# A spline layer on one Trainium2 core: two image tiles made one, and a masked sum moved from TensorE to GpSimd

## The chip, the cores and the metric

The kernel runs on one core of a Trainium2 chip. A core has four compute engines that work side by side and meet only through semaphores: PE (TensorE, matrix products into PSUM), DVE (VectorE), ACT (ScalarE) and POOL (GpSimd). SP (SyncE) starts DMAs. The metric is the device time of one whole execution in microseconds (us), smaller is better. Three runs of the kernel before took 19758.29, 19760.24 and 19772.59 us, a median of 19760.24 us.

## The reference, cut to what matters

The input `x` is (8, 64, 128, 128) in fp32. Four layers follow one another, each as `x = x + layer(group_norm(x))`. The first compares patches with weights by sums of absolute differences, the third is a wavelet convolution, the fourth replaces every pixel's 64 channels by the nearest of 512 vectors. The change is in the second, layer 1, a spline per channel:

```python
def _L1_conv_ref(x, coef, scale_base, scale_sp, bias):
    grid = _extended_grid(x.dtype)            # 12 knots, -2.2 to 2.2, 0.4 apart
    xcl = jnp.moveaxis(x, 1, -1)
    basis = _bspline_basis(xcl[..., None], grid)   # cubic, 8 functions
    spline = jnp.einsum('bhwck,ck->bhwc', basis, coef)
    out = scale_base * jax.nn.silu(xcl) + scale_sp * spline + bias
    return jnp.moveaxis(out, -1, 1)
...
x = x + _L1_conv_ref(_gn(x), L1_conv_coef, L1_conv_scale_base, L1_conv_scale_sp, L1_conv_bias)
```

## The kernel before, in words

Two images at a time make a pair: 128 partitions are 2 images of 64 channels. There are four pairs. Layer 0 of a pair is the bulk of the time; layers 2 and 3 of the pair before are threaded into layer 0 of the next one by a hand-written order. Layer 1 stands alone between two layer 0s (`run`, L1213), so it is a stage of its own, four times in the program. In the last pair, layers 2 and 3 follow it alone.

Inside layer 1 the order of instructions is not written out by hand. The framework orders them before the program runs, and each engine then works through its own queue in that fixed order. An instruction that waits holds back all that is behind it on its engine.

A stage handles 16 units (the loop at L719) of 8 rows, that is `N` = 1024 numbers per partition. For a unit:

- `xd` holds each image twice, on both halves of the partitions, as loaded by four DMAs from SP (L683). The lower half of the partitions serves three of six knots, the upper half the other three, so that one instruction makes two knots. For each of the two images ACT makes `z` = |2.5 (x - mean) / std| (L730), in a tile of 1024 columns.
- For each of three knot pairs `p` and each image `i`: `r` is the distance to the knot, cut at zero, made by ACT as a Relu (L739; `p` < 1 + `i`, which is three of the six) or by DVE as a min and a subtraction (L741; the other three, with the opposite sign). ACT squares it into `r3` (L742), and DVE multiplies `r3` by `r` (L743), which makes the cube.
- PE sums the cubes with the spline's coefficients into two PSUM tiles of 2 banks (L754): `pa` holds the part that counts everywhere, `pb` what is added where x is right of the mean. Each product has 64 output columns; the two images go to the two halves of the array and run side by side. A product in fp32 shows as two MATMUL instructions in the profile.
- ACT also makes `sl`, a Silu (L748), which PE adds to `pa` with the base scale (L756).

`end(n, pa, pb)` (L704) finishes a unit, called one unit late, at `p` = 1 of the next unit. DVE makes `u` = (x >= mean) * `pb` (L708). PE adds `u` to `pa` with two products by the identity, that is four instructions (L710). DVE then adds `pa`, the bias and `x` in place into `x` (L711). After every second unit DVE takes four `bn_stats` (L408) for the next group norm, and, but in the last pair, SP stores the chunk (L716).

PSUM has eight banks, all in use: `pa` and `pb` have two buffers of two banks. In SBUF, in buffers of 1024 columns: `z0` and `z1` two each, `r` three, `r3` five, `sl` two, `u` one.

Outside layer 1, POOL also copies borders between tiles in layer 2 of the last pair (L798, L799), while DVE does additions and subtractions there (L805 to L811).

Of the kernel before, what the change touches and what calls it, by code (L numbers as in the profile page):

```python
# [13 lines left out]
F32 = mybir.dt.float32  # L14
U32 = mybir.dt.uint32
AF = mybir.ActivationFunctionType
ALU = mybir.AluOpType
# [4 lines left out]
P = 128  # L22
# [8 lines left out]
NQ = 6  # L31
# [64 lines left out]
class Net:  # L96
# [568 lines left out]
    def layer1(self, mr, stats, store):  # L665
        nc, tc = self.nc, self.tc
        N = R * W // 2
        images = [slice(i * C, (i + 1) * C) for i in range(2)]
        with ExitStack() as ctx:
            sp = ctx.enter_context(tc.tile_pool(name="l1", bufs=2))  # L670
            xdp = ctx.enter_context(tc.tile_pool(name="l1_xd", bufs=3))
            cp = ctx.enter_context(tc.tile_pool(name="l1_c", bufs=1))
            pp = ctx.enter_context(tc.tile_pool(name="l1_ps", bufs=2, space=PSUM))

            def unit(n):
                return self.x[n // 2][:, n % 2 * R // 2 : (n % 2 + 1) * R // 2, :].rearrange("p r w -> p (r w)")

            def twice(n):

                xd = xdp.tile([P, 2, N], F32, name="xd")  # L680
                for i in range(2):
                    for h in range(2):
                        nc.sync.dma_start(out=xd[images[h], i, :], in_=self.x_of[0][images[i], n * N : (n + 1) * N])  # L683
                if n % 2 == 0:
                    self.x.append(self.load(n // 2))
                return xd

            l1w = cp.tile([P, L1W], F32, name="l1w")
            nc.sync.dma_start(out=l1w, in_=self.l1w_dram)
            dspl = l1w[:, 0 : 10 * C].rearrange("p (k n c) -> p k n c", k=2, n=5)  # L690
            dbase, of_image = l1w[:, 10 * C : 12 * C], l1w[:, 12 * C :].rearrange("p (i n) -> p i n", i=2)
            self.x = []
            xds = [twice(n) for n in range(3)]

            sb = cp.tile([P, 2], F32, name="sb")
            nc.vector.tensor_copy(sb[:, 0:1], mr[:, 1:2])
            nc.vector.tensor_scalar(sb[:, 1:2], mr[:, 0:1], mr[:, 1:2], -1.0, ALU.mult, ALU.mult)
            zb = cp.tile([P, 2, 2], F32, name="zb")
            for i in range(2):
                pm = pp.tile([P, 2, 512], F32, name="pm", tag="pa")  # L700
                nc.tensor.matmul(pm[:, 0, 0:2], of_image[:, i, :], sb, start=True, stop=True)
                nc.vector.tensor_scalar(zb[:, i, :], pm[:, 0, 0:2], 2.5, None, ALU.mult)

            def end(n, pa, pb):  # L704

                xv = unit(n)
                u = sp.tile([P, N], F32, name="u", bufs=1)
                nc.vector.scalar_tensor_tensor(u, xv, mr[:, 0:1], pb.rearrange("p q n -> p (q n)"), ALU.is_ge, ALU.mult)  # L708
                for q in range(2):
                    nc.tensor.matmul(pa[:, q, :], self.ident, u[:, q * 512 : (q + 1) * 512], start=False, stop=True)  # L710
                nc.vector.scalar_tensor_tensor(xv, pa.rearrange("p q n -> p (q n)"), self.bias1, xv, ALU.add, ALU.add)  # L711
                if n % 2 == 1:
                    j = n // 2
                    self.chunk_stats(stats, j)
                    if store:
                        nc.sync.dma_start(out=self.x_of[1][:, j * R * W : (j + 1) * R * W], in_=self.x[j].rearrange("p r w -> p (r w)"))  # L716

            late = None
            for n in range(2 * NCH):  # L719
                xv = unit(n)  # L720

                def work(name, bufs=2):
                    return sp.tile([P, N], F32, name=name, tag=name, bufs=bufs)

                pa = pp.tile([P, 2, 512], F32, name="pa")
                pb = pp.tile([P, 2, 512], F32, name="pb")
                zs = []
                for i in range(2):
                    z = work(f"z{i}")
                    nc.scalar.activation(z, xds[n][:, i, :], AF.Abs, bias=zb[:, i, 1:2], scale=zb[:, i, 0:1])  # L730
                    zs.append(z)
                for p in range(NQ // 2):
                    cubes, ws = [], []
                    for i in range(2):
                        r, r3 = work("r", 3), work("r3", 5)
                        kn = self.knots[:, p : p + 1]
                        on_act = p < 1 + i
                        if on_act:
                            nc.scalar.activation(r, zs[i], AF.Relu, bias=kn, scale=-1.0)  # L739
                        else:  # L740
                            nc.vector.tensor_scalar(r, zs[i], kn, kn, ALU.min, ALU.subtract)  # L741
                        nc.scalar.activation(r3, r, AF.Square)  # L742
                        nc.vector.tensor_tensor(r3, r3, r, ALU.mult)  # L743
                        cubes.append(r3)
                        ws.append(p + 3 if on_act else p)
                    if p == 0:
                        sl = work("sl")
                        nc.scalar.activation(sl, xv, AF.Silu, bias=sb[:, 1:2], scale=sb[:, 0:1])  # L748
                    for q in range(2):
                        cols = slice(q * 512, (q + 1) * 512)  # L750
                        for k, to in enumerate((pa, pb)):
                            for i in range(2):
                                stop = k == 1 and p == NQ // 2 - 1
                                nc.tensor.matmul(to[images[i], q, :], dspl[:, k, ws[i], :], cubes[i][:, cols], start=(p == 0), stop=stop)  # L754
                        if p == 1:
                            nc.tensor.matmul(pa[:, q, :], dbase, sl[:, cols], start=False, stop=False)  # L756
                    if p == 1 and late is not None:
                        end(*late)
                late = (n, pa, pb)
                if n + 3 < 2 * NCH:  # L760
                    xds.append(twice(n + 3))
                if n in range(4, 12, 2) and not store:
                    k = n // 2 - 2
                    nc.sync.dma_start(out=self.w2[:, k], in_=self.w2_dram[:, k])
            end(*late)

# [485 lines left out]
```

## Time and profile before

| what | us |
|---|---|
| median of three runs | 19760.24 |
| the profiled execution, its own time | 19757.03 |
| its span, first to last instruction | 19755.3 |
| PE busy in the span | 18769.1 |
| DVE busy | 18064.8 |
| ACT busy | 17182.7 |
| POOL busy | 2601.9 |
| layer 1, first to last product, pair 1 | 235.3 (3819.8 to 4055.1) |
| pair 2 | 238.8 (8699.2 to 8938.0) |
| pair 3 | 238.8 (13573.5 to 13812.3) |
| pair 4 | 236.1 (18435.9 to 18672.0) |

The four stages of layer 1 come to 949.0 us, 4.8% of the span; whatever the page says of busy shares over the span is mostly about layer 0, so layer 1 is read by windows of its own. A line of a group reads: line of the code, engine, operation, output <- inputs with their shapes, number, then busy time of the group in us and mean duration of one in ns, then how long the engine had been idle before and which instruction ended that. A line of the timeline reads: start in us, duration in us, engine, line, operation, and in brackets the idle time before it.

### The profile page before, as it was taken

How to read it: one execution, taken by the hardware profiler on the slowest of the kernel's cores; microseconds unless marked ns; L12 is line 12 of the kernel's file. 1: busy time of each engine (PE TensorE's matmuls, PEld its weight loads, DVE VectorE, ACT ScalarE, POOL GpSimd, SP SyncE). 2: the span in 40 equal slices, each digit the busy share in tenths (PEclk: the TensorE clock that was granted, in tenths of full speed). 3: DMA queues.
4: the chain of work that ended last, by engine and by line, in shares of the span. 5: the costliest groups of instructions: out<-in, count | busy, mean ns of one | idle time of the engine just before them, and what ended most of it. 6: DMA issues, size and time to landing. Idle time of an engine off the chain costs nothing. (4 is left out here: it accounts for less than half of the span.)

```text
span 19755.3 us, 326806 instructions
## 1 busy us (share of the span) xinstructions
PE 18769.1 (95%) x145178; PEld 5842.9 (30%) x145178; DVE 18064.8 (91%) x13865; ACT 17182.7 (87%) x6359; POOL 2601.9 (13%) x1726
## 2 busy tenths in 40 slices
PE   8999999999999999999999999999999999999898
PEld 2323323222222222222222222222222222222243
DVE  8999999989999899988999989998899999899837
ACT  7999999889899999988989999997999999999603
POOL 0000000000000333200000033310000003331004
PEclk9999999999999999999999999999999999999996
DMA  1000000211111000021111100002111110000101
GB/s 51 10 6 10 8 10 10 63 44 34 40 34 32 14 23 22 25 76 33 33 38 34 32 17 19 24 26 81 31 31 37 33 31 18 22 21 16 57 1 35
DMA packets 412631, 583.91 MB, mean 30 GB/s; under 512 B 64080, under 2 KB 309456, under 8 KB 385744
## 3 DMA queue, kind: packets, MB, share of 16 engines
q1 hardware_dynamic: 353872, 495.80, 8.4%
q0 software_dynamic: 57344, 67.21, 1.9%
q8 instruction: 1137, 18.63, 0.4%
q14 instruction: 278, 2.28, 0.0%
HBM read 439.55 MB, written 123.25 MB: 28 GB/s over the span
## 5 line engine op out<-in xcount | busy, mean ns | idle before, releaser
L589 ACT ACTIVATE buf<-buf,w 128x4096 f32<-128x4096 f32 x4272 | 15536.9, 3709 | 1277.6 <-PE ps L658 1071.4
L658 PE MATMUL ps<-buf,sel 128*32 128x512 f32 x126496 | 14140.7, 602 | 430.0 <-DVE buf L595 306.2
L591 DVE TENSOR_SCALAR buf<-buf,w 128x4096 f32<-128x4096 f32 x3634 | 8439.9, 2359 | 791.0 <-PE ps L658 782.9
L658 PEld LDWEIGHTS ps<-buf,sel 128*32 128x32 f32 x126496 | 3976.7, 111 | 10301.7 <-issue 8816.5
L595 DVE SCALAR_TENSOR_TENSOR buf<-buf,w,buf 128x2048 f32<-128x2048 f32 x2620 | 6052.6, 2349 | 49.3
L1150 POOL DMA_INDIRECT g<-in_L_conv_embed_weight,ix x768 | 1691.4, 2202 | 3282.8 <-issue 1965.3
L575 POOL DMA_DIRECT2D y<-in_x x512 | 594.1, 1954 | 10229.6 <-ACT y L563 8782.8
L1025 PE MATMUL cv<-dw,w2s 64*128 64x512 f32 x6912 | 1663.4, 610 | 10.5 <-issue 9.9
L1025 PEld LDWEIGHTS cv<-dw,w2s 64*128 64x128 f32 x6912 | 632.4, 188 | 1043.0 <-issue 1031.0
L1135 PE MATMUL pd<-embT,xn 64*128 64x512 f32 x1536 | 604.2, 661 | 166.6 <-DVE best L1147 166.6
L1002 DVE SCALAR_TENSOR_TENSOR dw<-sub,dws,dw 128x512 f32<-128x512 f32 (+2 forms) x768 | 574.6, 748 | 9.3
L1137 ACT ACTIVATE t<-esq_half,xsq 128x512 f32<-128x512 f32 x768 | 512.6, 711 | 71.2 <-DVE best L1147 71.2
L838 PE MATMUL ps<-dw,w 64*128 64x512 f32 x2304 | 525.7, 598 | 29.3 <-DVE dw L824 20.4
L1149 DVE FIND_INDEX8 ix<-best,nd 128x8 uint32<-128x512 f32 x768 | 526.1, 685 | 0.0
L743 DVE TENSOR_TENSOR r<-r,r 128x1024 f32<-128x1024 f32 x384 | 455.6, 1219 | 76.7 <-ACT r L742 76.7
L1147 DVE CUSTOM_DVE_ANT_0 nd<-pd,t 128x512 f32<-128x512 f32 x768 | 520.1, 677 | 0.0
L844 ACT ACTIVATE g<-ps,b2c 128x1024 f32<-128x1024 f32 x16 | 17.8, 1114 | 517.7 <-PE ps L838 517.7
L742 ACT ACTIVATE r<-r 128x1024 f32<-128x1024 f32 x384 | 385.3, 1045 | 93.9 <-PE pb L754 70.5
L754 PE MATMUL pa<-r,l1w 128*64 128x512 f32 x1536 | 426.2, 609 | 26.8 <-DVE r L743 26.8
L754 PE MATMUL pb<-r,l1w 128*64 128x512 f32 x1536 | 418.3, 598 | 0.0
L906 ACT ACTIVATE t<-esq_half,xsq 128x512 f32<-128x512 f32 x256 | 171.4, 714 | 239.0 <-DVE best L909 201.2
L1135 PEld LDWEIGHTS pd<-embT,xn 64*128 64x128 f32 x1536 | 163.3, 189 | 587.0 <-issue 305.5
(206 smaller groups left out, 5448.8 us busy)
## 6 DMA issues: line engine op xcount, KB each, us to landing
w2s<-w_dram SPq DMA_DIRECT2D x576, 192.0 KB
xd<-x_dram SPq DMA_DIRECT2D x256, 256.0 KB
x<-x_dram SPq DMA_DIRECT2D x56, 1024.0 KB
raw<-in_x SPq DMA_DIRECT2D x32, 1024.0 KB
y<-in_x POOLq DMA_DIRECT2D x512, 64.0 KB, 4.1
x_dram<-y SPq DMA_DIRECT2D x512, 64.0 KB
out<-x SPq DMA_DIRECT2D x32, 1024.0 KB
x_dram<-x SPq DMA_DIRECT2D x24, 1024.0 KB
```

The lines of the kernel that those rows point to most:

```text
L575: nc.gpsimd.dma_start(out=ys[p][at], in_=d, accum_op=ALU.add)
L589: nc.scalar.activation(ab, tap(j, ts[0]), AF.Abs, bias=w[:, ts[0] : ts[0] + 1], scale=-1.0)
L591: nc.vector.tensor_scalar(ab, tap(j, ts[0]), w[:, ts[0] : ts[0] + 1], None, ALU.max)
L595: nc.vector.scalar_tensor_tensor(at, tap(j, t, h), w[:, t : t + 1], at, ALU.max, ALU.add)
L658: nc.tensor.matmul(at, sel[:, M - 1 - m : 3 * M - 1 - m], rhs, start=(n == first[p]), stop=(n + 1 == first[p + 1]))
L754: nc.tensor.matmul(to[images[i], q, :], dspl[:, k, ws[i], :], cubes[i][:, cols], start=(p == 0), stop=stop)
L838: nc.tensor.matmul(ps[:, i], self.w2[rows, k, w, oab, :], v, start=(n == 0 and k == 0), stop=(n == 8 and k == 3))
L1002: nc.vector.scalar_tensor_tensor(out, v, wt, out, ALU.mult, ALU.add)
L1025: nc.tensor.matmul(ps[:, i], weights[r, w // 3, :], v, start=(k == 0 and n == 0), stop=(k == 3 and n == 8))
L1135: nc.tensor.matmul(ps, xns[j][at, r, :], self.embT[at, :], start=True, stop=True)
L1149: nc.vector.max_index(ix, mx, nd)
L1150: nc.gpsimd.indirect_dma_start(out=g[:, img, :], out_offset=None, in_=self.embed, in_offset=bass.IndirectOffsetOnAxis(ap=ix[:, 0:1], axis=0),)
```

## The change

Both images of a unit share one tile of 2 x 1024 = 2048 columns for `z`, `r` and `r3`. `z` is still made by two instructions, as the two images differ in scale. For `p` = 0 one Relu on ACT makes `r` for both images, for `p` = 2 one instruction on DVE; for `p` = 1 DVE makes image 0 and ACT image 1. One Square and one multiplication each serve both images. So the six squares and six multiplications of a unit become three and three, of twice the width; the three DVE distances become one of 1024 and one of 2048 columns, the three Relus one of 2048 and one of 1024.

The second part: PE's products of `u` with the identity (L710) go. In their place POOL adds `u` to `x` in SBUF, and the last DVE instruction of the unit takes `pa`, bias and this `x`. `end` is cut in two: `end` (mask, POOL's addition) at `p` = 1 of the next unit, `finish` (last addition, statistics, store) at `p` = 2.

Buffers: `z` two, `r` two and `r3` three of 2048 columns (`r3` two in the last pair), `sl` one.

```diff
@@ end @@
                 u = sp.tile([P, N], F32, name="u", bufs=1)
                 nc.vector.scalar_tensor_tensor(u, xv, mr[:, 0:1], pb.rearrange("p q n -> p (q n)"), ALU.is_ge, ALU.mult)
-                for q in range(2):
-                    nc.tensor.matmul(pa[:, q, :], self.ident, u[:, q * 512 : (q + 1) * 512], start=False, stop=True)
+                nc.gpsimd.tensor_tensor(xv, xv, u, ALU.add)
+
+            def finish(n, pa, pb):
+                xv = unit(n)
                 nc.vector.scalar_tensor_tensor(xv, pa.rearrange("p q n -> p (q n)"), self.bias1, xv, ALU.add, ALU.add)
...
                 def work(name, bufs=2):
-                    return sp.tile([P, N], F32, name=name, tag=name, bufs=bufs)
+                    return sp.tile([P, 2, N], F32, name=name, tag=name, bufs=bufs)
...
-                zs = []
+                z = work("z")
                 for i in range(2):
-                    z = work(f"z{i}")
-                    nc.scalar.activation(z, xds[n][:, i, :], AF.Abs, bias=zb[:, i, 1:2], scale=zb[:, i, 0:1])
-                    zs.append(z)
+                    nc.scalar.activation(z[:, i], xds[n][:, i, :], AF.Abs, bias=zb[:, i, 1:2], scale=zb[:, i, 0:1])
                 for p in range(NQ // 2):
-                    cubes, ws = [], []
-                    for i in range(2):
-                        r, r3 = work("r", 3), work("r3", 5)
-                        kn = self.knots[:, p : p + 1]
-                        on_act = p < 1 + i
-                        if on_act:
-                            nc.scalar.activation(r, zs[i], AF.Relu, bias=kn, scale=-1.0)
-                        else:
-                            nc.vector.tensor_scalar(r, zs[i], kn, kn, ALU.min, ALU.subtract)
-                        nc.scalar.activation(r3, r, AF.Square)
-                        nc.vector.tensor_tensor(r3, r3, r, ALU.mult)
-                        cubes.append(r3)
-                        ws.append(p + 3 if on_act else p)
+                    r, r3 = work("r"), work("r3", 3 if store else 2)
+                    kn = self.knots[:, p : p + 1]
+
+                    ws = [(p + 3, p + 3), (p, p + 3), (p, p)][p]
                     if p == 0:
-                        sl = work("sl")
+                        nc.scalar.activation(r, z, AF.Relu, bias=kn, scale=-1.0)
+                    elif p == 1:
+                        nc.vector.tensor_scalar(r[:, 0], z[:, 0], kn, kn, ALU.min, ALU.subtract)
+                        nc.scalar.activation(r[:, 1], z[:, 1], AF.Relu, bias=kn, scale=-1.0)
+                    else:
+                        nc.vector.tensor_scalar(r, z, kn, kn, ALU.min, ALU.subtract)
+                    nc.scalar.activation(r3, r, AF.Square)
+                    nc.vector.tensor_tensor(r3, r3, r, ALU.mult)
+                    if p == 0:
+                        sl = sp.tile([P, N], F32, name="sl", bufs=1)
                         nc.scalar.activation(sl, xv, AF.Silu, bias=sb[:, 1:2], scale=sb[:, 0:1])
...
-                                nc.tensor.matmul(to[images[i], q, :], dspl[:, k, ws[i], :], cubes[i][:, cols], start=(p == 0), stop=stop)
+                                nc.tensor.matmul(to[images[i], q, :], dspl[:, k, ws[i], :], r3[:, i, cols], start=(p == 0), stop=stop)
...
-                    if p == 1 and late is not None:
-                        end(*late)
+                    if p > 0 and late is not None:
+                        (end, finish)[p - 1](*late)
...
             end(*late)
+            finish(*late)
```

More of the change, by code (lines that the diff above doesn't have):

```diff
@@ L752, in layer1 @@
                             for i in range(2):
-                                stop = k == 1 and p == NQ // 2 - 1
-                                nc.tensor.matmul(to[images[i], q, :], dspl[:, k, ws[i], :], cubes[i][:, cols], start=(p == 0), stop=stop)
+                                stop = p == NQ // 2 - 1
+                                nc.tensor.matmul(to[images[i], q, :], dspl[:, k, ws[i], :], r3[:, i, cols], start=(p == 0), stop=stop)
                         if p == 1:
                             nc.tensor.matmul(pa[:, q, :], dbase, sl[:, cols], start=False, stop=False)
-                    if p == 1 and late is not None:
-                        end(*late)
+                    if p > 0 and late is not None:
+                        (end, finish)[p - 1](*late)
                 late = (n, pa, pb)
```

## The prediction, made before the changed kernel had run

> **What bounds the kernel now.** I began with the busy times of the page (PE 95% of the span, DVE 91%, POOL 13%), but these describe layer 0. The change touches layer 1 alone, so I asked for the windows of its four stages, first product to last:
>
> ```profile
> core 0: us, PE busy (x) PEld busy (x) DVE busy (x) ACT busy (x) POOL busy (x), PEclk, DMA share, GB/s
> 3819.80:4055.10 235.30, 234.02 (x886) 76.32 (x888) 199.04 (x202) 194.85 (x188) 0.00 (x0) 0.99 0.46 132
> 18435.90:18672.00 236.10, 235.81 (x888) 78.02 (x890) 198.75 (x202) 194.13 (x187) 0.00 (x0) 0.99 0.33 93
> ```
>
> PE is never idle, DVE and ACT are busy 84% and 83%, POOL not at all. In the timeline the first product with `sl` comes at 3901.51, 3915.94, 3930.72: a unit takes 14.43 or 14.78 us by turns. A window of eight whole units (116.5 us, 14.56 each) gives 100.87 us of DVE and 98.27 of ACT, 12.61 and 12.28 a unit. Its groups:
>
> ```profile
> L743 DVE TENSOR_TENSOR r<-r,r 128x1024 f32<-128x1024 f32 x48 | 56.8, 1219 | 5.0 <-ACT r L742 5.0
> L741 DVE TENSOR_SCALAR r<-z,knots 128x1024 f32<-128x1024 f32 x24 | 18.7, 807 | 0.0
> L710 PE MATMUL pa<-u,ident 128*128 128x512 f32 x32 | 15.0, 593 | 0.0
> L711 DVE SCALAR_TENSOR_TENSOR x<-pa,bias,x 128x1024 f32<-128x1024 f32 x8 | 10.3, 1284 | 11.1 <-PE pa L710 11.1
> ```
>
> Each unit has six cubes on DVE, three distances, and four PE instructions for `u`. DVE waits for the sum in L710, but has time to.
>
> **PE's part.** From the first L710 to the product behind it the timeline has 3905.39 to 3907.20 = 1.81 us. Without it a unit of PE is 14.56 - 1.81 = 12.75 us; the 24 products of cubes and two of `sl` stay. If PE still set the pace, 64 units would save 64 x 1.81 = 116 us. So what is late next decides.
>
> **DVE's part.** Two cubes back to back take 2.36 us; one of 2048 columns is 1.22 plus 1024 columns at the slope between a 512-wide and a 1024-wide TENSOR_TENSOR of layer 2 (0.680 and 1.214 us, 1.043 ns a column): 2.29. Three times 0.07 is 0.21 saved. Two distances take 1.53 in a row, one of 2048 columns as in L470 1.44: 0.09 saved. DVE: 12.61 - 0.30 = 12.31 us a unit. ACT: a 2048-wide Square takes 1.90 (L1119) where two take 1.99, so three save 0.27, the one wide Relu about 0.15: 11.9. By their work alone DVE and ACT would fit under 12.75.
>
> **POOL's part.** No row shows a two-input addition of 1024 columns on POOL. Below: it must write 1024 columns; MEMSETs of 256 and 2304 columns take 0.32 and 2.03 us, 0.836 ns a column, so about 0.96. Above: twice the rate of an undisturbed 256-column COPY (0.40 us, of which I call 0.11 fixed: 1.14 ns), 2.45; with the 0.55 that a one-column TENSOR_TENSOR (L466, a power) takes as the fixed part, 2.9. I take one COPY's rate plus one more access at 0.836, 1.98 ns x 1024 + 0.11 = 2.15, call it 2.2, nearest to the COPY rows since it reads as they do. The Trainium skill, "GPSIMD Engine Reference", section 3.1, gives 4497 ns for such an addition of 2048 columns; half, 2.25, is an estimate by that page, and by it the unit below would be 0.05 longer.
>
> Does it lie beside DVE's work? This is the timeline of layer 2, where POOL copies while DVE adds:
>
> ```profile
> 18742.57 1.22 DVE L805 TENSOR_TENSOR hs<-x 128x1024 f32<-128x1024 f32 x1
> 18742.72 2.47 POOL L798 COPY dw<-dw 128x256 f32<-128x256 f32 x1 [22.48 <-DVE dw L824]
> 18743.71 1.22 DVE L806 TENSOR_TENSOR hd<-x 128x1024 f32<-128x1024 f32 x1
> ...
> 18776.08 1.21 DVE L805 TENSOR_TENSOR hs<-x 128x1024 f32<-128x1024 f32 x1
> 18776.22 1.33 POOL L798 COPY sub<-sub 128x256 f32<-128x256 f32 x1 [1.81 <-DVE sub L811]
> 18777.21 1.41 DVE L806 TENSOR_TENSOR hd<-x 128x1024 f32<-128x1024 f32 x1
> ...
> 19028.03 0.40 POOL L798 COPY dw<-dw 128x256 f32<-128x256 f32 x1 [22.48 <-DVE dw L824]
> ```
>
> The same COPY takes 0.40 us with DVE quiet, 2.47 us while two TENSOR_TENSORs of DVE run (it ends 0.26 after the second), and 1.33 when it gets in between two, where the second takes 1.41 instead of 1.21. So they exclude each other, and whoever is second waits. A rule stands behind these rows (the Trainium skill, "SBUF — State Buffer", "Who interferes with whom"): a DVE instruction with two SBUF inputs, or in a two-port mode, keeps out a POOL instruction that reads SBUF for its whole length; one with a PSUM input does not. Taken strictly, POOL would get in when the first one ends; the first COPY above did not, so I count a lost turn as possible.
>
> **Where the addition falls.** Per unit DVE has three cubes (6.7 us), distances (0.72 + 1.36), `u`, L711's successor, and two `bn_stats` on average. The cubes are the form that the rows show to exclude POOL; that is enough here. When `u` ends, the next cube (p = 2) is ready, its square having run under the p = 1 cube and `u`, so it starts first and the addition waits 2.2 us for it. Behind this cube are the next unit's narrow distance and the last addition, which waits for POOL. Whichever wins the next turn, DVE gets nothing done for POOL's 2.2 us, plus about 0.1 for the hop back (L466's end to L696's start is 0.03, 18427.90 to 18427.93). Behind the waiting instruction stand the statistics and the next unit's first cube; PE waits for that, and SP's store and the `pa` buffer too. So the addition is not beside DVE's work but in line with it: 12.31 + 2.2 + 0.1 = **14.6 us** a unit, against 14.56. PE then idles 1.9 us a unit.
>
> Sum: 64 x 0.05 = +3 us. Start of a stage: now z, Relu, Square and cube follow in halves, first product 6.7 us after `z` begins (18429.20 to 18435.90); in wholes z 2.37, Relu 2.0, Square 1.9, cube 2.29 and the hops make 8.6: +1.9, four times +8. End: `u` to last addition was 56.62 to 59.98 = 3.36, becomes 1.28 + 2.2 + 0.15 = 3.6, four times +1. The rest costs nothing: loads come three units ahead (DMA share 0.46), the store leaves half a unit later into a queue that waits for nothing urgent, `sl` with one buffer is rewritten after PE's p = 1, which ends 3.4 us before the next unit begins. `pa` is freed at p = 2 instead of p = 1; PE needs it 3.4 us after that cube, and if this cover goes, PE waits for the same last addition that is in the sum already. Three `r3` buffers of double width exceed five single ones; two in the last pair tie a square to the product two steps before, a ring of 2 x (5.6 + 3.5 + 3.5) / 2 products and three squares with cubes at 4.35, 25.7 us for two units, below 29.2. Total +12 on 19757: **19769**, in terms of the median (3 us above the profiled run) 19772.
>
> **Rivals.**
> *Hidden (0.30).* The addition fits where DVE idles or runs something else than cubes, or costs DVE only what the second COPY did (0.2 us for 256 columns, 0.8 for 1024). Then a unit is PE's 12.75 to DVE's 13.2: -116 + 9 = -107, 19650, to -87 + 9, 19680; with POOL at 1.3 us (COPY's rate) and in line, 13.7: -55 + 9, 19711. For it: POOL is empty and nothing needs the sum for most of a unit. Against it: the rows above, and only 3.6 of DVE's 12.3 us are neither cube nor distance.
> *In line with waits on top (0.28).* With one wide tile, distance, Square and cube of a step follow strictly: 0.1 + 1.9 us in which DVE has nothing of that step to do, at p = 1 3.0 with ACT's Relu. Now the other image fills this (DVE waits only 5.0 us for squares in eight units). If the fixed order puts a cube straight behind its distance and POOL's addition elsewhere, a unit is 14.6 + 1 to 2: +64 to +128 + 9, 19830 to 19894. It decides from 0.6 us of such waits a unit. POOL at 2.9 alone is +45 + 12: 19814.
> *In line (0.42)*, my forecast: 2.2 give or take 0.5, 64 x 0.5 = 32: 19740 to 19802.
>
> A measurement of this kernel tells about 0.2%, 40 us or 0.62 us a unit. Hidden is faster; waits on top, slower; in line, within. The range takes in the likeliest case, nearly all of the hidden one and the lighter half of the other: 19650 to 19855.
>
> **What would show it.** POOL additions of 2 us or more, longer than that where a cube runs; in DVE's rows a wait for POOL before the last addition, near 2 us in each unit; PE idle for 1.5 to 2 us a unit before p = 0; units of 14.3 to 15. Units near 12.8 with PE full would prove the exclusion wrong; long DVE waits for squares would prove the second rival.

## The result, and the profile after

The changed kernel takes 19796.96 us (median of 20 runs), the kernel before 19763.0 in 20 runs taken beside them. The ratio is 1.0017, 95% interval 1.0010 to 1.0023: slower by about 34 us, inside the 0.2% that the prediction called no change, though the interval leaves out 1. The forecast was 19772, the range 19650 to 19855.

The four stages did not move together. "Start" is from DVE's first instruction of the stage (L696) to the first product, "products" from there to the end of the last one, "end" from there to the end of the last addition (before, the last unit's products by the identity count to the end); the numbers are read off the two traces, one execution each, in us.

| pair | start before | after | products before | after | end before | after | whole stage |
|---|---|---|---|---|---|---|---|
| 1 | 7.02 | 10.84 | 236.8 | 238.7 | 4.69 | 5.13 | +6.2 |
| 2 | 7.02 | 10.84 | 240.2 | 234.2 | 4.69 | 5.13 | -1.8 |
| 3 | 7.02 | 10.84 | 240.2 | 234.2 | 4.69 | 5.13 | -1.7 |
| 4 | 7.97 | 13.25 | 237.5 | 269.3 | 4.69 | 5.13 | +37.5 |

Together +40; the medians differ by 34. Nearly all of the loss is in the last pair's products.

The stages' windows in the changed kernel, in the columns that the prediction shows for before (stretch and length, busy us and number for PE, PE's weight loads, DVE, ACT and POOL, granted clock, DMA share, GB/s):

```profile
3824.80:4062.90 238.10, 217.46 (x830) 62.88 (x832) 205.84 (x138) 184.00 (x123) 57.75 (x15) 0.95 0.43 126
8712.40:8946.00 233.60, 212.85 (x830) 60.11 (x832) 190.42 (x138) 181.70 (x123) 66.51 (x15) 0.98 0.43 127
18447.70:18716.40 268.70, 222.24 (x830) 61.88 (x832) 207.88 (x138) 181.56 (x121) 57.65 (x15) 0.95 0.27 76
```

PE is no longer full: it idles 21 us in each of the first two windows shown and 46 in the last. No other engine took its place: in the second window DVE is busy 82%. So something waits. In pair 2, eight units (8774 to 8890), DVE's waits and ACT's longest are (who waited, for whom, us in total, times, longest):

```profile
DVE x L713 <- POOL x L709: 18.1, 8, 2.3
```
```profile
ACT r L744 <- DVE r L743: 21.8, 8, 2.8
```

L713 is the last addition of a unit (L711 before), L709 POOL's. Once in every unit DVE stands still for 2.27 us until POOL is done. The timeline of DVE and POOL there, one unit's end:

```profile
8803.04 1.27 DVE L708 SCALAR_TENSOR_TENSOR u<-x,mr,pb 128x1024 f32<-128x1024 f32 x1
8804.23 2.28 DVE L745 TENSOR_TENSOR r<-r,r 128x2048 f32<-128x2048 f32 x1
8804.46 4.29 POOL L709 TENSOR_TENSOR x<-x,u 128x1024 f32<-128x1024 f32 x1 [10.22 <-DVE u L708]
8808.78 1.28 DVE L713 SCALAR_TENSOR_TENSOR x<-pa,bias,x 128x1024 f32<-128x1024 f32 x1 [2.27 <-POOL x L709]
```

`u` ends, the cube starts, the addition starts 0.2 us behind it and takes 4.29 us, where the shortest of the 64 takes 2.34: it first waits for the cube. DVE, done with the cube at 8806.51, waits for the addition to 8808.75. This is the picture of the prediction. In pair 1 the framework put two cubes behind `u` in every second unit, and POOL got in between them:

```profile
3901.51 6.67 DVE L745 TENSOR_TENSOR r<-r,r 128x2048 f32<-128x2048 f32 x2
```
```profile
3901.73 4.30 POOL L709 TENSOR_TENSOR x<-x,u 128x1024 f32<-128x1024 f32 x1 [11.67 <-issue]
```

Two cubes take 4.48 us elsewhere; here 6.67. The same 2.2 us is paid as a stretched cube instead of a wait. In the units between, DVE waits for the addition as in pair 2.

In the last pair the units come to take 14.03 and about 20.2 us by turns, 17.1 on average once this has settled. DVE, POOL, ACT and PE in a long one:

```profile
18550.33 4.46 DVE L745 TENSOR_TENSOR r<-r,r 128x2048 f32<-128x2048 f32 x1
...
18559.53 0.81 DVE L740 TENSOR_SCALAR r<-z,knots 128x1024 f32<-128x1024 f32 x1
18563.40 2.29 DVE L745 TENSOR_TENSOR r<-r,r 128x2048 f32<-128x2048 f32 x1 [3.06 <-ACT r L744]
```
```profile
18549.30 3.33 POOL L709 TENSOR_TENSOR x<-x,u 128x1024 f32<-128x1024 f32 x1 [10.88 <-DVE u L708]
```
```profile
18554.83 2.00 ACT L738 ACTIVATE r<-z,knots 128x2048 f32<-128x2048 f32 x1 [0.20 <-DVE r L745]
18561.46 1.91 ACT L744 ACTIVATE r<-r 128x2048 f32<-128x2048 f32 x1 [4.63 <-PE pb L754]
```
```profile
18554.85 1.70 PE L754 MATMUL pa<-r,l1w 128*64 128x512 f32 x4 [3.17 <-DVE r L745]
18556.33 1.93 PE L754 MATMUL pb<-r,l1w 128*64 128x512 f32 x4
...
18560.33 1.03 PE L754 MATMUL pb<-r,l1w 128*64 128x512 f32 x4
```

ACT has the distance ready at 18556.83 and waits 4.63 us for products of PE before it may square. A square reads nothing that PE makes; it waits because it writes into an `r3` whose products are not done. The last pair has two `r3` buffers. These products are late and also slow: PE has waited 3.17 us for the stretched cube, and in the 3.1 us from 18554.8 the granted clock is 0.56. Four instructions take 1.93 us there and 1.03 a little later, and from 18554.85 to the next product behind `sl` (18559.42) PE needs 4.57 us, where the same sequence in pair 2 takes 2.93 (8803.17 to 8806.10), at a clock of 1.00.

### The profile page after: what moved, and what is told of

Same layout as the page of the kernel before. It is cut to its first block, busy times and chain, and to the rows that moved or that the text cites. A ratio compares the mean times of both kernels' runs of the same rounds, so it can differ in the third digit from the quotient of the medians.

```text
span 19802.0 us, 325783 instructions
## 1 busy us (share of the span) xinstructions
PE 18675.1 (94%) x144922; PEld 5775.7 (29%) x144922; DVE 18066.7 (91%) x13609; ACT 17148.2 (87%) x6103; POOL 2866.8 (14%) x1790
## 5 line engine op out<-in xcount | busy, mean ns | idle before, releaser
L745 DVE TENSOR_TENSOR r<-r,r 128x2048 f32<-128x2048 f32 x192 | 466.7, 2442 | 78.8 <-ACT r L744 78.8
L744 ACT ACTIVATE r<-r 128x2048 f32<-128x2048 f32 x192 | 362.9, 1900 | 127.0 <-DVE r L743 73.5
L709 POOL TENSOR_TENSOR x<-x,u 128x1024 f32<-128x1024 f32 x64 | 257.7, 4027 | 779.4 <-DVE u L708 551.2
```

## The experiments

Three questions: is it the number of `r3` buffers that slows the last pair; which part of the change costs; and does POOL cost because it and DVE exclude each other, or because DVE waits for it.

**Three `r3` buffers in the last pair** (`e1_r3_three`). To make room in SBUF, the loads of that pair give up a buffer.

```diff
-            xdp = ctx.enter_context(tc.tile_pool(name="l1_xd", bufs=3))
+            xdp = ctx.enter_context(tc.tile_pool(name="l1_xd", bufs=3 if store else 2))
-                    r, r3 = work("r"), work("r3", 3 if store else 2)
+                    r, r3 = work("r"), work("r3", 3)
```

> The changed kernel, but the last pair too has three buffers for r3 (to make room, its loads xd have two instead of three). Theory, the ring: in the last pair a square waits for PE's products of two steps before, as it shares their buffer, and this wait makes its units 17.1 us instead of 14.6. Then the last stage falls from 269 us of products to about 234, as in pairs 2 and 3, and the time by 35 us to the time before the change, a ratio of 1.000 (0.9990 to 1.0005). Rival, something else is slow in the last pair (the loads of the next layer's weights, eight chunks of x held at once): the stage stays at 265 us or more and the ratio at 1.0015 or more.

Measured: 19764.12 against 19767.49, ratio 0.9999 (0.9990 to 1.0008). The last stage's products fall from 269.3 to 235.5 us; the others read 240.2, 234.3, 234.3. The missing buffer is the whole loss that was measured; with it no difference from the kernel before can be told.

**Two in all pairs** (`e2_r3_two`): `work("r3", 2)` and nothing else.

> The changed kernel with two buffers for r3 in all four pairs. The ring theory: the first three stages become like the last, about 269 us of products instead of 239, 234 and 234, so about +100 us over the changed kernel, 19895 us, a ratio of 1.0067 to the kernel before. If the last pair is slow for a reason of its own, nothing changes: 1.0017.

Measured: 19913.53, ratio 1.0074 (1.0060 to 1.0088). All four stages read 268.4 to 269.8 us, with the same turns of about 14 and 20 us. Each stage by itself reproduces it, so the last pair has no reason of its own.

**Wide tiles alone** (`e3_wide_only`): PE adds `u`, the unit ends in one piece.

```diff
-                nc.gpsimd.tensor_tensor(xv, xv, u, ALU.add)
-
-            def finish(n, pa, pb):
-                xv = unit(n)
+                for q in range(2):
+                    nc.tensor.matmul(pa[:, q, :], self.ident, u[:, q * 512 : (q + 1) * 512], start=False, stop=True)
...
-                    if p > 0 and late is not None:
-                        (end, finish)[p - 1](*late)
+                    if p == 1 and late is not None:
+                        end(*late)
```

> One part of the change alone: tiles of 2048 columns, but PE adds u as before and the unit ends in one piece; POOL has nothing to do. r3 has three buffers, in the last pair two. Theory, that POOL's addition stands in line with DVE and is what sets the unit at 14.6 to 15.2: PE sets the pace again, units of 14.6 us in the first three stages with no DVE wait of 2 us before the last addition, stages of products of 233 to 237 us, the start 4 us later as in the changed kernel, and a last stage at least as long as the 269 us of the changed kernel, as the ring has 1.8 us more of PE in it: 265 to 295. Together 19800 to 19835. Rival, that wide tiles by themselves make waits: units of 15.2 or more in all stages, DVE waiting over 1 us a unit for squares.

Measured: 19752.98, ratio 0.9993 (0.9984 to 1.0002), so not told from no change. Units are 14.43 us in the first three stages, but for the first unit, with PE full: 231.6 to 232.0 us of products, which pays for the later start. The surprise is the last stage: two `r3` buffers, units of 14.78, 237.3 us. My ring theory as stated for this run (265 to 295) was wrong: two buffers cost 0.35 us a unit here, against 2.5 with POOL's addition.

**POOL's addition alone** (`e4_pool_only`): tiles, buffers and distances of the kernel before, its `end` cut in two as in the change.

> The other part alone: tiles of 1024 columns with all buffers as before, POOL adds u, the end of a unit in two pieces. Theory, in line: DVE's 12.6 us and POOL's 2.3 us and a hop of 0.1 exclude each other, units of 15.0 us, 0.45 more than before, so +29 us over four equal stages with no later start: about 19792, a ratio of 1.0015. Rival, that narrow cubes leave POOL enough turns and it is hidden: units of 12.8, 19650, a ratio of 0.994.

Measured: 19843.59, ratio 1.0039 (1.0025 to 1.0052), +76 us where I expected +29. Units run from 13 to 22 us and are 16 on average. In pair 2:

```profile
8804.54 3.39 DVE L745 TENSOR_TENSOR r<-r,r 128x1024 f32<-128x1024 f32 x1
```
```profile
8804.03 2.82 POOL L709 TENSOR_TENSOR x<-x,u 128x1024 f32<-128x1024 f32 x1 [12.12 <-ACT r L741]
```

Here POOL is first and a cube of 1.21 us takes 3.39. Around it DVE waits for PE, and PE's weight loads for cubes (in 220 us of pair 2, 11.2 and 36.3 us). So, in the orders that the framework found, narrow tiles bear POOL worse than wide ones. Why 16 and not 15, I did not settle.

**Nobody adds `u`** (`e5_no_add`): as `e1_r3_three` without L709; the part right of the mean is left out of the result.

> As the run with three r3 buffers in every pair, but nobody adds u: DVE still makes it, and the part right of the mean is left out of the result. It shows what is left when POOL's addition costs nothing. By the sum in the prediction: PE 12.75 us a unit, DVE 12.3, so units of 12.7 to 12.8, stages of products of 204 to 207 us, -117 us over 64 units and +16 for the later starts: about 19665, a ratio of 0.995. If waits between wide squares and cubes matter besides POOL, units are 13.5 or more and the time 19715 or more.

Measured: 19644.08, ratio 0.9941 (0.9925 to 0.9956). Units of 12.71 us almost throughout, PE full, 206.6 to 209.0 us of products. The unit that the sum gave for PE held to 0.05 us; with three `r3` buffers POOL's addition costs all that PE's products had cost. The time is 21 us below the expected one: the end of a stage takes 2.65 us instead of 4.69, and its first unit is shorter too, neither of which I had counted.

**POOL writes but does not read** (`e6_pool_writes`):

```diff
-                nc.gpsimd.tensor_tensor(xv, xv, u, ALU.add)
+                end.u = u
+                for c in (N, N, N // 2):
+                    nc.gpsimd.memset(u[:, 0:c], 0.0)
...
-                nc.vector.scalar_tensor_tensor(xv, pa.rearrange("p q n -> p (q n)"), self.bias1, xv, ALU.add, ALU.add)
+                nc.vector.scalar_tensor_tensor(xv, pa.rearrange("p q n -> p (q n)"), end.u[:, 0:1], xv, ALU.add, ALU.add)
```

> As the run before, but POOL fills u with zeros three times (1024, 1024 and 512 columns, by the MEMSET rows about 2.4 us in all) where it added u, and DVE's last addition waits for that; POOL reads nothing. The part right of the mean is left out. Theory, that POOL and DVE exclude each other only where both read SBUF: the fills run beside DVE's cube, which keeps 2.28 us, DVE waits 0.2 to 0.6 us for POOL, units of 12.8 to 13.2, 19670 to 19700. Rival, that any POOL instruction is in line with DVE: 14.6 us a unit, a wait near 2.3 us before the last addition, 19760.

Measured: 19669.48, ratio 0.9954 (0.9939 to 0.9969). Most units take 12.71, a few 13.1 to 14.7. DVE and POOL in one unit (in this kernel L747 is the cube, L742 the narrow distance, L715 the last addition, L711 the fills):

```profile
8827.21 2.28 DVE L747 TENSOR_TENSOR r<-r,r 128x2048 f32<-128x2048 f32 x1
8829.53 0.97 DVE L742 TENSOR_SCALAR r<-z,knots 128x1024 f32<-128x1024 f32 x1
8830.42 1.26 DVE L715 SCALAR_TENSOR_TENSOR x<-pa,u,x 128x1024 f32<-128x1024 f32 x1
```
```profile
8827.41 2.54 POOL L711 MEMSET u<- 128x1024 f32 x3 [12.53 <-DVE u L708]
```

The fills run beside the cube, which keeps its 2.28 us, and are done 0.5 us before the last addition. The rule of the Trainium skill that the prediction drew on ("SBUF — State Buffer", "Who interferes with whom") says as much: a cube's second input keeps out a POOL instruction that reads SBUF, not one that only writes. This run agrees.

In 12 of the 64 units DVE does wait for the fills, 30.9 us in all; where they fell beside a wide distance (8799.12), they took 3.62 us and DVE waited 2.52. So the dependency costs little where nothing on DVE holds POOL back. One thing was not kept equal: in the units looked at, a distance or a second cube stands ahead of the last addition, which in the changed kernel's pair 2 comes straight behind the cube.

**The sum unread, first try** (`e7_pool_unread`): `nc.gpsimd.tensor_tensor(u, xv, u, ALU.add)`, the part right of the mean left out.

> As the run with three r3 buffers in every pair, but POOL writes the sum of x and u into u, so that DVE's last addition need not wait for it; the part right of the mean is left out of the result. POOL reads as much as in the changed kernel. Theory, that the two exclude each other: POOL's 2.1 us of reading come out of DVE's time wherever they fall, one cube a unit is stretched from 2.28 to about 4.3 us, units of 14.3 to 14.6, 19750 to 19770. Rival, that only the wait of the last addition costs: units of 12.8, as without the addition, 19665.

Measured: 19760.67, ratio 0.9999 (0.9990 to 1.0008). It tells nothing apart: the last addition writes the `x` that POOL reads, so it still waits, 2.27 us as before.

**POOL beside DVE** (`e9_pool_beside`), the same question asked again: `nc.gpsimd.tensor_tensor(u, u, u, ALU.add)`.

> As the run with POOL's sum unread, mended: there DVE's last addition still waited, since POOL was reading the x that it writes. Now POOL adds u to itself in u, touches no x, and no DVE instruction waits for it but the next unit's u, half a unit or more later. The part right of the mean is left out of the result. Theory, exclusion: no wait before the last addition, but once a unit a cube or another DVE instruction is stretched by about 2 us, units of 14.2 to 14.6, 19745 to 19770. Rival, only the wait of the last addition cost: units of 12.71, as without any addition, 19645 to 19655.

Measured: 19646.94, ratio 0.9942 (0.9925 to 0.9958), the same as with no addition at all, units of 12.71. My theory falls, and the rival stands. DVE and POOL in a unit:

```profile
8810.93 2.28 DVE L745 TENSOR_TENSOR r<-r,r 128x2048 f32<-128x2048 f32 x1
8813.13 1.27 DVE L713 SCALAR_TENSOR_TENSOR x<-pa,bias,x 128x1024 f32<-128x1024 f32 x1
8814.32 1.19 DVE L740 TENSOR_SCALAR r<-z,knots 128x1024 f32<-128x1024 f32 x1
```
```profile
8811.09 3.87 POOL L709 TENSOR_TENSOR u<-u 128x1024 f32<-128x1024 f32 x1 [8.84 <-DVE u L708]
```

POOL still waits for the cube (3.87 us against 1.89 for the shortest), so the exclusion is there. But then it runs while DVE does the last addition, which reads PSUM and keeps its 1.27 us; in this unit only the narrow distance is stretched, 0.80 to 1.19. The order on DVE is that of the changed kernel's pair 2. (Reading `u` twice takes POOL 0.45 us less than `x` and `u`; that does not make up 2.27.) In the changed kernel this very addition is what waits for POOL, so there is nothing left to run beside it.

**DVE adds `u`, wide tiles** (`e8_wide_dve`): as `e1_r3_three` with `nc.vector.tensor_tensor(xv, xv, u, ALU.add)`; nothing left out.

> The changed kernel with three r3 buffers in every pair, and DVE itself adds u to x instead of POOL; nothing is left out. A TENSOR_TENSOR of 1024 columns costs DVE 1.14 us in a row of others, so 12.3 + 1.15 = 13.45 us a unit against POOL's 2.1 us of exclusion and a wait: units of 13.4 to 13.7, -55 to -75 us and +16 for the later starts: 19710 to 19730, a ratio of 0.9972 to 0.998. Rival, that DVE then has too little room and its fixed order makes it wait for squares: units of 14.4 or more, no gain, 19765.

Measured: 19688.08 against 19761.75, ratio 0.9963 (0.9949 to 0.9976), faster than expected and than both kernels. Units go 12.71, 12.71, 14.68, 14.34; products 217.2 to 219.0 us. DVE now does more and waits less: 106.25 us busy in 108, and in that window it waits only 0.7 us for squares and 0.7 for PE.

**DVE adds `u`, narrow tiles** (`e10_narrow_dve`): `e4_pool_only` with the same line.

> The tiles of 1024 columns and the buffers of the kernel before, the unit's end in two pieces, and DVE adds u to x. Nothing is left out. By rows DVE has 12.6 + 1.14 = 13.75 us a unit and PE 12.75: 64 x -0.8 = -52 us with no later start, 19710, a ratio of 0.9974. Rival: narrow tiles made DVE wait on top when POOL added (units near 16 instead of 15), so units of 14.5 or more and no gain, 19760.

Measured: 19742.83, ratio 0.9991 (0.9981 to 1.0000). Units of 12.8 to 17.1, products 233.4 to 237.8 us. Neither number came out; the size is nearer the rival's, and as the interval reaches 1.0000 even the direction is barely told. With DVE this full, wide tiles are worth some 55 us (19742.83 less 19688.08; the two ratios' intervals lie apart), each in the order that the framework found for it.

**No addition and two `r3` buffers** (`e11_no_add_r3_two`), the part right of the mean left out.

> Nobody adds u (the part right of the mean is left out) and r3 has two buffers in all pairs. It asks whether the ring of two buffers costs by itself or only together with POOL. By the prediction's sum the ring is 25.7 us for two units, 12.85 a unit: units of 12.7 to 13.1, 19645 to 19670. Rival, the ring itself is longer than summed: units of 14 to 17, 19730 to 19920.

Measured: 19731.38, ratio 0.9987 (0.9977 to 0.9996). Units of 14.03 and 14.34 by turns, against 12.71 with three buffers. The ring by itself is 28.37 us for two units, not the 25.7 that I had summed.

**One more distance from DVE to ACT** (`e12_wide_dve_act`): `e8_wide_dve` with `p < 2` on ACT for both images.

```diff
-                    ws = [(p + 3, p + 3), (p, p + 3), (p, p)][p]
-                    if p == 0:
+                    ws = [(p + 3, p + 3), (p + 3, p + 3), (p, p)][p]
+                    if p < 2:
                         nc.scalar.activation(r, z, AF.Relu, bias=kn, scale=-1.0)
-                    elif p == 1:
-                        nc.vector.tensor_scalar(r[:, 0], z[:, 0], kn, kn, ALU.min, ALU.subtract)
-                        nc.scalar.activation(r[:, 1], z[:, 1], AF.Relu, bias=kn, scale=-1.0)
```

> As the run with wide tiles and DVE's addition (19688 us, units of 12.71 to 14.68, 13.6 on average, DVE the fullest), but the last narrow distance of DVE goes to ACT, which makes both images of p = 1 with one Relu. Nothing is left out. DVE falls by 0.75 us a unit to 12.7, ACT rises by 0.9 to 12.8, PE has 12.71. Theory, DVE sets the pace: units of 12.8 to 13.2, 64 x -0.4 to -0.8: 19635 to 19662. Rival, three engines this evenly full stall one another: units of 13.6 or more, 19688 or more.

Measured: 19701.83, ratio 0.9968 (0.9956 to 0.9980), no gain over `e8_wide_dve`, which is the rival's number. The stages differ: 208.2 us of products in pair 4, with units of 12.71 and 13.09, 214.2 in pair 1, but 228.6 and 228.7 in pairs 2 and 3, with 13.09 and 15.6 by turns. Pairs 1 to 3 run the same code, and pair 4 differs only in buffers, the store and a load. The order on DVE and ACT is the same in pairs 2 and 3 and another in pairs 1 and 4; which difference in it does it was not tried.

## Why the prediction was right, and where it was not

*PE's part* held. Without the products by the identity a unit of PE is 12.71 us (predicted 12.75), seen wherever nothing else sets the pace (`e5_no_add`, `e9_pool_beside`).

*DVE's part* held. In pair 2 DVE is busy 98.30 us in eight units of 116.60, 12.29 a unit; predicted 12.31. A cube of 2048 columns takes 2.28 us (predicted 2.29).

*POOL's part*: 2.34 us undisturbed, predicted 2.2; the estimate by the Trainium skill ("GPSIMD Engine Reference", section 3.1), 2.25, was nearer.

*Where the addition falls* held in pairs 2 and 3: behind a cube, DVE idle for 2.27 us (predicted 2.2 and 0.1 for the hop), units of 14.57 (predicted 14.6, before 14.56). The place, the wait and the sum are those of the prediction. The reason given beside it was too broad. I wrote that POOL is "not beside DVE's work but in line with it", as if exclusion alone made the sum 12.31 + 2.2. It takes both together: POOL held back by a cube, and nothing behind that cube which can run while POOL reads. Take the cube's exclusion away (`e6_pool_writes`, with the reservation made there) or the wait (`e9_pool_beside`), and the unit is near 12.71. So the sign that I had named, that units near 12.8 "would prove the exclusion wrong", was not one: `e9_pool_beside` has such units, and the exclusion is there. Where POOL gets in ahead of a cube, the cube pays instead (pair 1, `e4_pool_only`). Pair 1 comes to 15.15 us a unit by its other order: there PE waits 2.35 us for a cube in every second unit, the granted clock in the 3.1 us behind that is 0.57, and DVE then waits 1.27 us for `pb`, which is the 0.6 a unit. That the lower clock makes this wait is read off the rows, not tried.

*The last pair's two buffers* is the step that failed. The prediction costed them at nothing, since "a ring" of "25.7 us for two units" is "below 29.2". Two things were wrong. The ring itself is 28.37 us (`e11_no_add_r3_two`): I had counted work and short hops on it, but, as I take it, not the places where DVE and ACT have something else in their queues when the ring needs them; I did not follow it row by row. That alone would have cost nothing, as 28.37 is still below 29.2. What failed is that I compared the ring with the unit as if the two were apart. POOL's addition lies on the ring: a cube stretched to 4.46 delays its products, these the next square in their buffer, that its cube; the two units become 34.2. Of the 5.85 us more, the stretched cube of the one unit (2.2) and DVE's wait for POOL in the other (2.27) make about 4.5, as the rows read. The rest is near the 1.6 us that PE loses at the lower clock in the long unit, which the prediction did not have; in `e11_no_add_r3_two` the clock stays at 1.00. With PE's addition, two buffers cost 0.35 us a unit (`e3_wide_only`); with nobody's, 1.5; with POOL's, 2.5. Three buffers removed it (`e1_r3_three`).

*The start* to the first product was mis-sized: +8 us predicted, 3 x 3.82 + 5.28 = +16.7 measured. The order of ACT, which the sum did not have, is part of the difference. In the last pair:

```profile
18435.68 2.37 ACT L731 ACTIVATE z<-xd,zb 128x1024 f32<-128x1024 f32 x2 [17.60 <-DVE zb L702]
18438.07 1.28 ACT L748 ACT_TABLE_LOAD   x1
18439.36 1.24 ACT L748 ACTIVATE sl<-x,sb 128x1024 f32<-128x1024 f32 x1
18440.51 1.99 ACT L738 ACTIVATE r<-z,knots 128x2048 f32<-128x2048 f32 x1
18442.40 1.13 ACT L741 ACTIVATE r<-z,knots 128x1024 f32<-128x1024 f32 x1
18443.44 3.69 ACT L744 ACTIVATE r<-r 128x2048 f32<-128x2048 f32 x2
```

The second distance comes before the first square in all pairs (1.1 us), and in the last one the table load and the Silu too (2.5). In the other three I also took the wrong time for before: the 6.7 us from `z` to the first product hold in the last pair, and the others have 5.8. But most of the later start came back at once: from the first product to the first with `sl` the four stages take 2.6, 4.1, 4.3 and 1.6 us less than before, 12.6 in all. Start and first unit together cost +4.1.

*The end*: +0.44 us a stage, +0.3 predicted.

*The sum*: products +3 predicted; measured +1.9, -6.0, -6.0 and +31.8, that is +21.7, the first three a gain of 10 and the last a loss that was not foreseen. Between the first and the last unit's products with `sl`, the pairs' own pace, the change is +6.2, -1.1, -0.4 and +35.1; so the gain in pairs 2 and 3 is mostly the first unit's, and the loss is the last pair's ring and, for a small part, pair 1's order. The forecast of no change beyond 0.2% came out, but that the total stayed there is in part luck: only one pair of four has two buffers, and with two in all of them the time is 19913.53 (`e2_r3_two`), outside the range.

*Rivals.* "Hidden" did not happen, though its floor of 12.75 us is real. "In line with waits on top" did, in the last pair, by another mechanism than the one that I gave: not a cube straight behind its distance, but squares waiting for a buffer.

## What to carry to other kernels

In these runs, work handed to an idle engine was free only where the busy engine had something to run meanwhile that neither needed the result nor was excluded: look at what stands in the other queue just behind it, and ask for each instruction whether it excludes or waits. Here DVE did the addition itself for 1.2 us and was faster by 0.4% than the kernel before, where handing it to an engine that was 0% busy in the stage gained nothing. And a buffer count is judged on the ring that it closes, with every wait of the new schedule on it, not by the engines' work: a ring 12% below the unit on paper cost 0.17% of the whole kernel.

## What the runs showed of the hardware that I had not expected

An addition of 1024 columns on POOL took 2.34 us with two tiles read and 1.89 with the same tile read twice. POOL's fills do not disturb a two-input cube on DVE, but a one-input distance of 1024 columns beside them took 0.97 instead of 0.80 us. An instruction of DVE with one input in PSUM ran at its full 1.27 us beside POOL's addition. After PE had waited 3.17 us (last pair) and 2.35 us (pair 1) the granted clock was 0.56 and 0.57 in the next 3.1 us, and a matrix instruction took up to 1.06 us instead of 0.59; in eight units of pair 2 (8774 to 8890), where PE waits 1.6 us at most, the clock stayed at 1.00. And the same code took 214.2 us of products in pair 1 and 228.6 in pair 2, with another fixed order of the framework's on DVE and ACT (`e12_wide_dve_act`).
